# Two softmax roots as one GpSimd power each, and a new instruction order, in a block-attention residual kernel

## The chip, the cores and the metric

One core of a Trainium2 chip runs the whole program. The metric is the device time of one execution in microseconds (us). The engines are PE (TensorE), DVE (VectorE), ACT (ScalarE), POOL (GpSimd) and SP (SyncE, which here only issues DMAs).

## The reference, cut to what matters

The input x has 8 batches of 512 rows of 1024 numbers. Each batch is cut into 8 blocks of 64 rows.

```python
blk   = x.reshape(8, 8, 64, 1024).sum(axis=2)             # block sums
keys  = einsum('bnh,kh->bnk', blk, Wk)
keys  = keys / sqrt(mean(keys**2) + 1e-6) * rms_weight    # the root that is changed
attn  = softmax(einsum('bnh,h->bn', keys, cond[1]))       # over the 8 blocks
p     = einsum('bn,bnh->bh', attn, blk) @ Wo.T            # one row for each batch
y     = x + p
out   = x + (y - mean(y)) / sqrt(var(y) + 1e-6) * gamma + beta
```

## The kernel before

**Tiling.** The 8 batches go through in three groups of 2, 4 and 2 (GROUPS). In a group every partition holds whole rows of x, two in a tile x of 128x2x1024, so that "row k" (0 to 31) is one 128x1024 piece: rows 0 to 7 are group 0, rows 8 to 23 group 1, rows 24 to 31 group 2. Nine units (UNITS) of 2 or 4 rows share their statistics; U0 to U7 compute theirs on POOL, U8 on the other engines.

**Steps of a group's attention.** `bs` sums blocks on PE; `col` transposes the sums on DVE; `proj n.0` multiplies by Wk and `proj n.1` by Wo on PE. `sm n` is the softmax of group n: `sq` (ACT) and `qk` (DVE) read the projection, `sdd` spreads the two sums over 8 columns, a small matmul adds them over partitions, `v` writes the variance `cv` (128x8), then comes the inverse root `ca`, the score `sc`, the maximum `mx`, the exponential `ex0` on ACT, the reciprocal `rc` and the weights `wc`. `v n w` scales the second projection by them, `p n mm` spreads it over the partitions, two copies `cp0` and `cp1` make the tile pb, and four small DMAs put rows of it into tab.

**Steps of a row.** `S` (L646, DVE) adds p to x and sums the row; `Q` (L648, ACT) gives its sum of squares. On POOL a unit's `v`, `std` and `rs` (L692, L695, L715; std and rs are powers), and `s2`, `sd2` fill a tile stat that PE transposes (`U mm`) and ACT or DVE copies to `lt`. `D` (L746, DVE) writes (gamma + std) x y into one of three pairs of PSUM banks (t0, t1, t2), `R` (L732, PE, two rows in one step) adds the terms that depend on mean, beta and p there, and `E` (L761, ACT) scales the pair by rs back into x, which frees it for the third D after it. Each pair of rows is then stored, 1 MB; the last four rows go out singly.

**The root before.** `inverse_root` takes a logarithm (`ln`) and an exponential (`ex`) on ACT and then a Newton step: `n1` on POOL (on DVE in group 0), `n2` and `n3` on DVE.

**The order.** All steps are collected in a list with their dependences, and the string ORDER is the order in which they are emitted, with the engine (a, b, c after a step's number) and the PSUM bank (after the colon) of each. Engines run their own instructions in that order. Words like f1:7 emit matmuls of zeros that fill a bank ahead of a D or keep PE busy; z and h words add zeros to a bank in use. x and the weights are loaded through 14 tile slots on SP's queue in the order of LOADS, gamma (`gam`) behind group 1's rows.

Of the kernel before, what the change touches and what calls it, by code (L numbers as in the profile page):

```python
# [130 lines left out]
def block_attn_resid_kernel(  # L131
# [91 lines left out]
    umv = [alloc(f"umv{i}", [P, MAXU, 2]) for i in range(NU)]  # L223
    ubn = alloc("ubn", [P, 2, 2, 6])
    pmv = [alloc(f"pmv{i}", [P, 4]) for i in range(2)]
    kw = alloc("kw", [P, QU], BF16) if junk is None else junk[:, :QU]
# [5 lines left out]
        [alloc(f"{n}{i}", [P, MAXU]) for i in range(NU)] for n in ("ussq", "uv", "u0", "ua", "urs", "usx", "ustd")  # L232
# [213 lines left out]
    def project(G, which):  # L446

        n = G["n"]
        b = blkT[n % 2]
        name = f"proj{n}.{which}"  # L450
        w = wT[which].rearrange("p c (q j k) -> p c j q k", j=4, k=HB)
        if (n, which) in PARTS:
            at = 0
# [450 lines left out]
```

## Time and profile before

| | |
|---|---|
| median of 3 runs | 146.02 us (145.58 to 146.04) |
| profiled execution | 144.9 us |
| its span, first to last instruction | 143.2 us |
| mean granted TensorE clock | 0.932 |
| busy: PE, DVE, ACT, POOL | 78%, 67%, 64%, 41% |
| moved by DMA | 42.76 MB, 299 GB/s over the span |

The profiled execution is 1.7 us longer than its span and 1.1 us shorter than the median. The shares are means over stages with different limits, so they have to be read stage by stage: loading and group 0 up to 56 us, the attention of group 1 up to 73.6 us, then the rows up to 138 us and the last stores.

### The profile page before, as it was taken

Reading aid. Unit: us, or ns where it says so; the run is one execution under the profiler, and the core shown is the slowest. Engines: PE = TensorE matmul, PEld = TensorE weight load, DVE = VectorE, ACT = ScalarE, POOL = GpSimd, SP = SyncE. Lnnn points to the kernel's source line nnn. Section 1 sums busy time; section 2 is a strip of 40 time slices with the busy share of each in tenths; the row PEclk is TensorE's granted clock in tenths of the full one; section 3 lists DMA queues with packets and bytes.
Section 4 is the critical chain, followed back from the end, with each engine's and each line's share of the span. In section 5 each row is a group of like instructions: output and inputs, shape, how many; then the busy total and the mean of one; then the engine's idle time right before and its main releaser. Section 6 shows DMA issues by size and latency. Waiting matters only on the chain.

```text
span 143.2 us, 2871 instructions
## 1 busy us (share of the span) xinstructions
PE 112.3 (78%) x1093; PEld 58.9 (41%) x1101; DVE 95.5 (67%) x161; ACT 90.9 (64%) x140; POOL 58.5 (41%) x107
## 2 busy tenths in 40 slices
PE   7869853989999685999693989989798498496820
PEld 2539652947985222544340335443252132122300
DVE  3040312311315996928879999999999999997930
ACT  3022520024931898255689989899989989989630
POOL 6888800000000066652000895566506928809100
PEclk9995999599999999999999599999999869999965
DMA  4999999999999999605499870724770850775993
GB/s 126 427 413 422 413 409 414 410 411 423 426 410 424 410 413 420 263 0 238 204 307 417 314 295 5 293 89 204 291 298 6 347 240 0 295 293 220 411 401 145
DMA packets 7526, 42.76 MB, mean 299 GB/s; under 512 B 808, under 2 KB 808, under 8 KB 3672
## 3 DMA queue, kind: packets, MB, share of 16 engines
q1 hardware_dynamic: 7440, 42.54, 73.5%
q8 instruction: 8, 0.13, 0.4%
q10 hardware_dynamic: 72, 0.04, 0.1%
q14 instruction: 6, 0.05, 0.1%
HBM read 25.73 MB, written 16.78 MB: 297 GB/s over the span
## 4 chain that ended last, share of the span: by engine, by line
DMA 33%; PE 24%; DVE 17%; ACT 11%; issue 6%; POOL 3%; SPq 2%; DVEq 0%; ACTq 0%
PE b L473 11%; DVE t L746 9%; DMA gam<-in_L_cond_ln_gamma_dram 8%; DMA x<-in_L_cond_Wo_dram 8%; DMA x<-in_L_cond_Wk_dram 6%; DMA x<-in_x_dram 5%; PE t L732 5%; PE t L407 4%; ACT x L761 4%; DVE x L646 4%; ACT square L648 3%; DMA tab<-in_L_cond_ln_gamma_dram 3%; DMA pb<-in_cond_dram 3%; ACT woT L241 2%; PE b L429 1%
## 5 line engine op out<-in xcount | busy, mean ns | idle before, releaser
L746 DVE SCALAR_TENSOR_TENSOR t<-gam,ustd,x 128x1024 f32<-128x1024 f32 x31 | 39.1, 1291 | 3.7 <-ACT x L761 2.5
L648 ACT ACTIVATE square<-x,tot 128x1024 bf16<-128x1024 f32 x32 | 36.7, 1147 | 3.3 <-DVE x L646 2.1
L646 DVE SCALAR_TENSOR_TENSOR x<-x,pb 128x1024 f32<-128x1024 f32 x32 | 37.6, 1223 | 0.1
L761 ACT ACTIVATE x<-t,urs 128x1024 f32<-128x1024 f32 x31 | 33.2, 1107 | 5.5 <-PE t L732 2.4
L700 POOL TENSOR_SCALAR stat<-tot 128x8 f32<-128x8 f32 (+1 forms) x8 | 7.5, 934 | 53.1 <-DVE x L646 53.0
L732 PE MATMUL t<-tab,lt 32*128 32x512 f32 x124 | 24.9, 667 | 4.8 <-DVE lt L243 2.2
L407 PE MATMUL t<-ident,x 128*128 128x128 f32 x120 | 17.9, 316 | 5.3 <-DMA x<-in_L_cond_Wk_dram 3.0
L869 PE MATMUL b<-zeros 128*128 128x512 bf16 (+1 forms) x57 | 18.2, 439 | 2.1 <-DVE zeros L294 1.0
L407 PEld LDWEIGHTS t<-ident,x 128*128 128x128 f32 x120 | 16.9, 202 | 6.6 <-issue 4.7
L869 PEld LDWEIGHTS <-zeros 128*128 128x128 bf16 x87 | 8.7, 108 | 17.2 <-issue 12.8
L695 POOL TENSOR_TENSOR ustd<-uv,halfs 128x4 f32<-128x4 f32 (+1 forms) x8 | 13.3, 1660 | 5.5 <-DVE uv L692 4.1
L732 PEld LDWEIGHTS t<-tab,lt 32*128 32x128 f32 x124 | 7.5, 191 | 16.9 <-DVE t L746 5.7
L241 ACT COPY wkT<-t 128x1024 f32<-128x1024 f32 x5 | 5.1, 1013 | 14.1 <-PE t L407 14.1
L715 POOL TENSOR_TENSOR urs<-uv,halfs 128x4 f32<-128x4 f32 (+1 forms) x8 | 13.2, 1650 | 0.0
L243 DVE COPY wkT<-t 128x1024 f32<-128x1024 f32 x3 | 3.7, 1225 | 12.1 <-PE t L407 12.1
L429 PE MATMUL b<-x,blk 128*32 128x256 f32 x128 | 8.4, 384 | 4.2 <-DMA x<-in_x_dram 3.7
L473 PE MATMUL b<-wkT,blkT 128*32 128x256 f32 x192 | 11.0, 380 | 0.6 <-DVE blkT L439 0.6
L241 ACT COPY woT<-t 128x1024 f32<-128x1024 f32 x6 | 5.8, 1014 | 7.8 <-PE t L407 7.8
L429 PE MATMUL t<-x,blk 128*32 128x256 f32 x128 | 7.9, 382 | 3.1 <-DMA x<-in_x_dram 3.1
L473 PEld LDWEIGHTS b<-wkT,blkT 128*32 128x32 f32 x192 | 5.9, 110 | 5.8 <-issue 1.2
L473 PE MATMUL b<-woT,blkT 128*32 128x256 f32 x128 | 7.9, 382 | 0.0
L869 PE MATMUL t<-zeros 128*128 128x512 bf16 x22 | 6.4, 380 | 1.1 <-ACT lt L241 0.6
(94 smaller groups left out, 101.8 us busy)
## 6 DMA issues: line engine op xcount, KB each, us to landing
x<-in_x_dram SPq DMA_DIRECT2D x16, 1024.0 KB
out_dram<-x SPq DMA_DIRECT2D x14, 1024.0 KB
x<-in_L_cond_Wk_dram SPq DMA_DIRECT2D x4, 1024.0 KB
x<-in_L_cond_Wo_dram SPq DMA_DIRECT2D x3, 1024.0 KB
out_dram<-x SPq DMA_DIRECT2D x3, 512.0 KB
x<-in_L_cond_Wo_dram SPq DMA_DIRECT2D x2, 512.0 KB
gam<-in_L_cond_ln_gamma_dram SPq DMA_DIRECT2D x1, 512.0 KB
out_dram<-x SPq DMA_DIRECT2D x2, 256.0 KB
```

Source lines behind the costliest of these rows:

```text
L241: nc.scalar.copy(dst, src)
L407: nc.tensor.transpose(half(part, c // 4)[:, bass.ts(c % 4, P)], tile_of(name)[:, e % RT, c::HC], ident)
L429: nc.tensor.matmul(bank(f"bs{n}")[32 * j : 32 * j + 32, :QU], blk[G["g"]], tile_of(name)[:, r, bass.ts(j, QU)], start=(t == 0 and r == 0), ...
L473: nc.tensor.matmul(bank(name)[32 * j : 32 * j + 32, :QU], b[:, c, :], w[:, c, j], start=(c == 0), stop=(c == HC - 1),)
L646: add(f"S{k}", [(DVE, 1.15)], lambda e: nc.vector.scalar_tensor_tensor(x_row(k), x_row(k), 1.0, pb[n], ALU.mult, ALU.add, accum_out=total) ...
L648: add(f"Q{k}", [(ACT, 1.28)], lambda e: nc.scalar.activation(square, x_row(k), AF.Square, bias=total, scale=-float(H), accum_out=ssq), rea ...
L695: add(f"{T} std", [(POOL, 0.5 + 0.16 * U)], lambda e: nc.gpsimd.tensor_tensor(std, v, halfs[:, :1].to_broadcast([P, U]), ALU.pow), reads=[ ...
L715: add(f"{T} rs", [(POOL, 0.5 + 0.16 * U)], lambda e: nc.gpsimd.tensor_tensor(rs, v, halfs[:, 1:].to_broadcast([P, U]), ALU.pow), reads=[V, ...
L732: nc.tensor.matmul(half(f"row{k}", h), lts[q % NST][lo : lo + 32, r // RT, :], tab_of(k)[0][lo : lo + 32, :], start=False, stop=True, skip ...
L746: add(f"D{k}", [(DVE, 1.21)], lambda e: nc.vector.scalar_tensor_tensor(flat(pair(name)), gam, std, x_row(k), ALU.add, ALU.mult), reads=["g ...
L761: add(f"E{k}", [(ACT, 1.13)], lambda e: nc.scalar.activation(x_row(k), flat(pair(name)), AF.Identity, scale=rs), reads=[RS], writes=[xk(k) ...
L869: nc.tensor.matmul(bank_at(i)[:, :n], zeros, zeros[:, 0:1].to_broadcast([P, n]), start=start, stop=True, skip_group_check=True)
```

## The change

In groups 1 and 2 the five steps of the inverse root become one step `pow` on POOL: cv to the power -0.5, a 128x8 tensor against a constant of -0.5. Group 0 keeps the old root. Beside this, scratch tiles are shared: `diag` and the scratch output `kw` (bf16 before) become parts of the tile vw0 (f32), and the tiles u0 and ua, which only U8 uses, exist once. The other new branches of the code (kinds "a" and "d", BY_PE, DIVIDE) are not taken with the constants given. ORDER is new as a whole.

```diff
+ROOT_POW = (1, 2)
+DIVIDE = False
 ORDER = (
-    "0 2 3 65:0 1 104 4 66:1 95 5 110 67:2 6 99 7 68:3 103 8 9 10 11 12 13 14 15 17 16 18 19 20 21 22 23 24 f11:7 "
+    "1 3 65:0 95 2 4 104 66:1 100 5 0 112 67:2 6 97 7 68:3 8 9 10 11 12 13 14 15 17 16 18 19 20 21 22 23 24 f11:7 "
...
-    diag = alloc("diag", [P, 32])
...
+    diag = vw[0][:, :32]
...
-    kw = alloc("kw", [P, QU], BF16) if junk is None else junk[:, :QU]
+    kw = vw[0]
...
-            reads=["qw"], writes=["sd1"], use=keys)
+            reads=["qw"], writes=["sd1", "vw0"], use=keys)
...
-        inverse_root(T, cv, c0, ca, ca, ("cv", "c0", "ca", "ca"))
+        if n in ROOT_POW:
+            add(f"{T} pow", [(POOL, 2.0)], lambda e: nc.gpsimd.tensor_tensor(
+                ca, cv, halfs[:, 1:].to_broadcast([P, NBLK]), ALU.pow), reads=["cv", "halfs"], writes=["ca"])
+        else:
+            inverse_root(T, cv, c0, ca, ca, ("cv", "c0", "ca", "ca"))
```

Three places show how the order moves. The first is DVE in the softmax of group 1, from the variance to the first rows of group 1 (x12, x13); before:

```order
L507 TENSOR_SCALAR cv_123<-b0_82 128x8
L746 SCALAR_TENSOR_TENSOR t1_80<-gam_102,ustd1_155,x6_69 128x1024
L487 SCALAR_TENSOR_TENSOR ca_126<-ca_126,cv_123 128x8
L489 SCALAR_TENSOR_TENSOR ca_126<-ca_126,c0_125 128x8
L510 SCALAR_TENSOR_TENSOR cs_124<-b0_82,ca_126 128x8
L512 TENSOR_REDUCE mx_127<-cs_124 128x1
L746 SCALAR_TENSOR_TENSOR t2_81<-gam_102,ustd1_155,x6_69 128x1024
L243 COPY lt1_104<-b0_82 128x256
L515 RECIPROCAL es_128<-es_128 128x1
L516 SCALAR_TENSOR_TENSOR kw_120,wcol_129<-cs_124,es_128,diag8_90 128x8
L746 SCALAR_TENSOR_TENSOR t0_79<-gam_102,ustd1_155,x8_71 128x1024
L746 SCALAR_TENSOR_TENSOR t1_80<-gam_102,ustd1_155,x8_71 128x1024
```

and the same place of the change, one row further down:

```order
L798 SCALAR_TENSOR_TENSOR t1_80<-gam_101,ustd1_136,x6_69 128x1024
L523 SCALAR_TENSOR_TENSOR cs_115<-b0_82,ca_117 128x8
L525 TENSOR_REDUCE mx_118<-cs_115 128x1
L798 SCALAR_TENSOR_TENSOR t2_81<-gam_101,ustd1_136,x6_69 128x1024
L529 RECIPROCAL es_119<-es_119 128x1
L530 SCALAR_TENSOR_TENSOR vw0_106,wcol_120<-cs_115,es_119,diag8_89 128x8
L544 TENSOR_SCALAR vw0_106<-b1_83,wcol_120 128x256
L798 SCALAR_TENSOR_TENSOR t0_79<-gam_101,ustd1_136,x8_71 128x1024
L252 COPY pb1_108<-b0_82 128x4x128
L692 SCALAR_TENSOR_TENSOR x12_75,tot0_96<-x12_75,pb1_108 128x1024 x2
L798 SCALAR_TENSOR_TENSOR t1_80<-gam_101,ustd1_136,x8_71 128x1024
```

The two Newton steps and the copy of lt1 are gone from DVE; the scaling of vw0 and one half of pb1, which ACT did, have come to it; and the last D of group 0 (row 7, x8 into t1) stands behind the first two S of group 1.

The second place is POOL around the softmax of group 2; before (ca is the Newton product, uv0, ustd0 and stat0 belong to unit U4):

```order
L501 TENSOR_TENSOR sdd_122<-diag8_90,sd_121 128x16
L700 TENSOR_SCALAR stat0_95<-tot0_97 128x8
L486 TENSOR_TENSOR ca_126<-c0_125 128x8
L692 TENSOR_SCALAR uv0_134<-ussq0_130 128x4
L695 TENSOR_TENSOR ustd0_154<-uv0_134,halfs_87 128x4
L715 TENSOR_TENSOR urs0_146<-uv0_134,halfs_87 128x4
L710 TENSOR_TENSOR stat0_95<-ustd0_154,ind4_100 128x8x5
```

and with the change:

```order
L752 TENSOR_SCALAR stat0_94<-tot0_96 128x8
L510 TENSOR_TENSOR sdd_113<-diag8_89,sd_112 128x16
L519 TENSOR_TENSOR ca_117<-cv_114,halfs_87 128x8
L743 TENSOR_SCALAR uv0_125<-ussq0_121 128x4
L746 TENSOR_TENSOR ustd0_135<-uv0_125,halfs_87 128x4
L762 TENSOR_TENSOR stat0_94<-ustd0_135,ind4_99 128x8x5
L767 TENSOR_TENSOR urs0_131<-uv0_125,halfs_87 128x4
```

The power stands where the Newton product stood, ahead of U4's own variance and powers, on which the D of row 16 waits.

The third place is ACT near the end, from the last Q on; before:

```order
L648 ACTIVATE square_112,ussq0_130<-x4_67,tot0_97 128x1024
L761 ACTIVATE x9_72<-t1_80,urs2_148 128x1024
L484 ACTIVATE u00_138<-uv0_134 128x2
L485 ACTIVATE u00_138<-u00_138 128x2
L761 ACTIVATE x11_74<-t2_81,urs2_148 128x1024
L761 ACTIVATE x11_74<-t0_79,urs2_148 128x1024
L241 COPY lt1_104<-b0_82 128x128
```

and with the change:

```order
L813 ACTIVATE x10_73<-t0_79,urs2_133 128x1024
L694 ACTIVATE square_111,ussq0_121<-x4_67,tot0_96 128x1024
L742 ACTIVATE uv0_125<-ussq0_121,least_88 128x2
L493 ACTIVATE u00_129<-uv0_125 128x2
L813 ACTIVATE x11_74<-t2_81,urs2_133 128x1024
L494 ACTIVATE u00_129<-u00_129 128x2
L813 ACTIVATE x11_74<-t1_80,urs2_133 128x1024
```

The E of row 25 now stands ahead of the last Q (x4, row 31) and no longer behind it, U8's variance has come to ACT, and U7's lt copy has gone to DVE.

## Rows read from the trace of the kernel before

**Rows 1.** Stages: window, length, busy us of PE, PEld, DVE, ACT, POOL; clock, DMA share, GB/s.

```profile
56.14:73.64 17.50, 15.72 (x191) 7.29 (x194) 12.88 (x23) 9.97 (x20) 5.31 (x5) 1.00 0.54 200
73.64:97.00 23.36, 19.43 (x230) 8.81 (x227) 23.02 (x38) 21.66 (x36) 13.24 (x13) 0.93 0.61 248
...
110.00:128.00 18.00, 13.38 (x56) 4.58 (x56) 17.97 (x26) 16.88 (x24) 11.44 (x10) 0.91 0.57 234
```

**Rows 2.** Timeline of DVE, group 1's softmax: start, duration, instruction, [idle before].

```profile
56.14 0.69 DVE L352 TENSOR_SCALAR gam<-gam 128x1024 f32<-128x1024 f32 x1 [1.10 <-DMA gam<-in_L_cond_ln_gamma_dram]
...
62.50 0.42 DVE L498 SCALAR_TENSOR_TENSOR kw<-b,qw 128x256 bf16<-128x256 f32 x1 [1.74 <-ACT square L496]
...
65.39 0.16 DVE L507 TENSOR_SCALAR cv<-b 128x8 f32<-128x8 f32 x1
...
67.51 0.17 DVE L510 SCALAR_TENSOR_TENSOR cs<-b,ca 128x8 f32<-128x8 f32 x1
...
68.38 1.29 DVE L746 SCALAR_TENSOR_TENSOR t<-gam,ustd,x 128x1024 f32<-128x1024 f32 x1 [0.51 <-ACT x L761]
69.58 0.42 DVE L243 COPY lt<-b 128x256 f32<-128x256 f32 x1
69.91 0.15 DVE L515 RECIPROCAL es<-es 128x1 f32<-128x1 f32 x1
...
72.44 1.29 DVE L746 SCALAR_TENSOR_TENSOR t<-gam,ustd,x 128x1024 f32<-128x1024 f32 x1 [0.89 <-ACT x L761]
73.64 1.22 DVE L646 SCALAR_TENSOR_TENSOR x<-x,pb 128x1024 f32<-128x1024 f32 x1
```

**Rows 3.** Timeline of ACT: group 1's two pb copies; the E of rows 10 and 11.

```profile
72.30 1.06 ACT L241 COPY pb<-b 128x512 f32<-128x512 f32 x2
...
93.00 2.12 ACT L761 ACTIVATE x<-t,urs 128x1024 f32<-128x1024 f32 x2 [0.51 <-PE t L732]
```

**Rows 4.** Timeline of POOL: the Newton products, and powers of 4 and 2 columns.

```profile
66.11 0.89 POOL L486 TENSOR_TENSOR ca<-c 128x8 f32<-128x8 f32 x1 [3.27 <-ACT c L485]
...
96.94 0.20 POOL L486 TENSOR_TENSOR ca<-c 128x8 f32<-128x8 f32 x1 [1.40 <-ACT c L485]
...
98.39 1.97 POOL L695 TENSOR_TENSOR ustd<-uv,halfs 128x4 f32<-128x4 f32 x1
...
129.08 0.72 POOL L695 TENSOR_TENSOR ustd<-uv,halfs 128x2 f32<-128x2 f32 x1 [4.14 <-DVE uv L692]
```

**Rows 5.** Timeline of DVE from group 2's softmax on.

```profile
96.97 1.29 DVE L746 SCALAR_TENSOR_TENSOR t<-gam,ustd,x 128x1024 f32<-128x1024 f32 x1 [0.32 <-PE t L869]
98.17 0.16 DVE L487 SCALAR_TENSOR_TENSOR ca<-ca,cv 128x8 f32<-128x8 f32 x1
98.25 1.22 DVE L646 SCALAR_TENSOR_TENSOR x<-x,pb 128x1024 f32<-128x1024 f32 x1
...
106.62 0.69 DVE L243 COPY pb<-b 128x512 f32<-128x512 f32 x1
107.22 1.22 DVE L646 SCALAR_TENSOR_TENSOR x<-x,pb 128x1024 f32<-128x1024 f32 x1
```

**Rows 6.** Timeline of PE: the fills ahead of group 1's projection; 32 matmuls of group 2's second one.

```profile
57.24 1.03 PE L869 MATMUL t<-zeros 128*128 128x512 bf16 x4 [0.32 <-DVE blkT L439]
...
92.89 1.93 PE L473 MATMUL b<-woT,blkT 128*32 128x256 f32 x32
```

**Rows 7.** The end: ACT's E of rows 25, 26 and 27; SP's store of rows 24 and 25; DMA by windows.

```profile
128.62 1.10 ACT L761 ACTIVATE x<-t,urs 128x1024 f32<-128x1024 f32 x1
...
129.96 2.10 ACT L761 ACTIVATE x<-t,urs 128x1024 f32<-128x1024 f32 x2
...
129.75 0.33 SPq L813 DMA_DIRECT2D out_dram<-x  x1
...
130.00:131.00 1.00, 0.89 (x6) 0.45 (x5) 1.00 (x1) 1.00 (x3) 0.97 (x2) 1.00 0.57 238
...
140.00:141.00 1.00, 0.00 (x0) 0.00 (x0) 0.00 (x0) 0.00 (x0) 0.00 (x0) 0.50 0.87 334
```

More of the change, by code (lines that the diff above doesn't have):

```diff
@@ L231, in block_attn_resid_kernel @@
     ussq, uv, u0, ua, urs, usx, ustd = (
[L232 removed]
+        [alloc(f"{n}{i}", [P, MAXU]) for i in range(k)] * (NU // k) if k else [None] * NU for n, k in (
+            ("ussq", NU), ("uv", NU), ("u0", 1), ("ua", NU if "b" in UKIND else 1), ("urs", NU),
+            ("usx", NU if set(UKIND) & set("pa") else 0), ("ustd", NU))
     )
@@ L388, in table @@
                 out=t[32 * q + 2 : 32 * q + 2 + g, :], in_=p[0:P:w, i * HALF : (i + 1) * HALF]),
-                reads=[f"pb{n % 2}.{j}" for j in range(2)], writes=[f"tab{n % NTAB}.{q}"], mb=0.01)
+                reads=[f"pb{n % NPB}.{j}" for j in range(2)], writes=[f"tab{n % NTAB}.{q}"], mb=0.01)
         if (n, "x") in TABS:
@@ L464, in project @@
                     add(f"{name}.{at}.{c0}.{qs}.{cs}", [(PE, 0.012 * cs + 0.108 * qs * cs)], lambda e, go=go: go(),
-                        reads=[f"blkT{n % 2}"] + w_keys(which, range(2 * at, 2 * (at + qs)), halves[0]),
+                        reads=[f"blkT{n % NBT}"] + w_keys(which, range(2 * at, 2 * (at + qs)), halves[0]),
                         claim=("b", name) if at == c0 == 0 else None, use=[] if at == c0 == 0 else [name])
@@ L477, in project @@
             add(f"{name}.{c0}", [(PE, 0.98)], lambda e, go=go: go(),
-                reads=[f"blkT{n % 2}"] + w_keys(which),
+                reads=[f"blkT{n % NBT}"] + w_keys(which),
                 claim=None if c0 else ("b", name), use=[name] if c0 else [])
@@ L536, in spread_out @@
             add(f"{part} cp{i}", [(ACT, 0.6), (DVE, 0.69)], lambda e, i=i: copy(
-                e, bands(pb[n % 2])[:, :, i, :], half(part, i).rearrange("p (q d) -> p q d", d=P)),
-                reads=[("slot", part)], writes=[f"pb{n % 2}.{i}"], release=part)
+                e, bands(pb[n % NPB])[:, :, i, :], half(part, i).rearrange("p (q d) -> p q d", d=P)),
+                reads=[("slot", part)], writes=[f"pb{n % NPB}.{i}"], release=part)
     def spread_p(G, part, start):
@@ L644, in moments, with go @@
                 reads=[S], writes=[Q], use=y, release=[y, y])
+        elif kind in "ad":
+            if place[k][1] % RT == 0:
+                tile_ = x_name(k)
+                add(f"A{k}", [(POOL, ADD_ISSUE)], lambda e: nc.gpsimd.dma_start(
+                    out=tile_of(tile_), in_=pb[n].unsqueeze(1).to_broadcast([P, RT, H]), accum_op=ALU.add),
+                    reads=p_keys, writes=[xk(k), xk(k + 1)], mb=ADD_MB)
+            if kind == "a":
+                add(f"Q{k}", [(ACT, 1.34)], lambda e: nc.scalar.activation(
+                    square, x_row(k), AF.Square, bias=total, scale=-float(H), accum_out=ssq), reads=[xk(k), S], writes=[Q])
+            else:
+                b = ubn[:, k % 2]
+                add(f"B{k}", [(DVE, 1.3)], lambda e: both_halves(b, x_row(k)), reads=[xk(k)], writes=[f"ubn{k % 2}"])
+                add(f"C{k}", [(DVE, 0.2)], lambda e: nc.vector.bn_aggr(out=umv[u][:, r, :], in_=b),
+                    reads=[f"ubn{k % 2}"], writes=[f"umv{u}.{r}"])
+        elif k in BY_PE:
+            y = f"y{k}"
+            def go():
+                for h in range(2):
+                    nc.tensor.matmul(pair(y)[:, h, :].rearrange("p (q d) -> p q d", d=P), ident, bands(x_row(k))[:, :, h, :],
+                                     start=True, stop=False, skip_group_check=True)
+                spread_p(G, y, False)
+            add(f"Y{k}", [(PE, 2.75)], lambda e: go(), reads=["ident", xk(k), "vw0", f"spread{g}"], claim=("t", y))
+            add(f"V{k}", [(ACT, 1.3)], lambda e: nc.scalar.activation(
+                bands(x_row(k)).rearrange("p q i d -> p i q d"), pair(y).rearrange("p i (q d) -> p i q d", d=P),
+                AF.Identity, accum_out=total), writes=[xk(k), S], use=y, release=[y, y])
+            add(f"Q{k}", [(ACT, 1.28)], lambda e: nc.scalar.activation(
+                square, x_row(k), AF.Square, bias=total, scale=-float(H), accum_out=ssq), reads=[xk(k), S], writes=[Q])
         else:
@@ L685, in unit @@
                 a, umv[u][:, :U, 1], UP * UP, pmv[n][:, 2:3], ALU.mult, ALU.add),
-                reads=[f"umv{u}.{r}" for r in range(U)] + [f"pmv{n}.2"], writes=[f"ua{u}"])
+                reads=[f"umv{u}.{r}" for r in range(U)] + [f"pmv{n}.2"], writes=[A])
             add(f"{T} vc", [(E, c)], lambda e: engine[e].tensor_scalar(v, ssq, 2.0 / H * UP * UP, 0.0, ALU.mult, ALU.add),
                 reads=Q4, writes=[V])
-            add(f"{T} v", [(E, c)], lambda e: engine[e].tensor_tensor(v, v, a, ALU.add), reads=[f"ua{u}"], writes=[V])
+            add(f"{T} v", [(E, c)], lambda e: engine[e].tensor_tensor(v, v, a, ALU.add), reads=[A], writes=[V])
+        elif UKIND[q] == "d":
+            add(f"{T} v", [(E, c), (DVE, 0.18)] if slow else [(E, c)], lambda e: engine[e].tensor_scalar(
+                v, umv[u][:, :U, 1], UP * UP, EPS * UP * UP, ALU.mult, ALU.add),
+                reads=[f"umv{u}.{r}" for r in range(U)], writes=[V])
         else:
```

74 lines of the change are left out of this document (43 added, 31 removed), and 40 rows, old and new, of the table ORDER.

## The prediction

> **What bounds the kernel now.** I read the windows by stage first, then the timelines of DVE, ACT and POOL in the stages that the change touches, then the end. Up to 56 us the kernel loads; the stage ends with DVE idle for 1.10 us until gamma has landed [rows 2]. From there to 73.64 us DVE is busy 12.88 us of 17.50 and PE 15.72 [rows 1]: the softmax of group 1 is a chain through PE and ACT, and DVE waits in it, 1.74 us before `qk`, 0.51 and 0.89 us before two D [rows 2]. From 73.64 us on DVE has hardly a gap: 23.02 us busy of 23.36, 17.97 of 18.00, with ACT at 21.66 and 16.88 [rows 1]. Here a microsecond of DVE work is a microsecond of time. At the end DMA takes over: the store of rows 24 and 25 is issued at 129.75 us, when their last E (128.62, 1.10 long) is done; the DMA engines are at work from about 130.4 us (0.57 of the window from 130 to 131) to about 140.9 (0.87 of that from 140) [rows 7]. The stores from there on are 4 MB, 4.19 million bytes in 10.5 us or 0.4 MB per us, so they run without a pause. The store of rows 26 and 27 can be issued when its E ends at 129.96 + 2.10 = 132.06, and the MB ahead of it is through at about 130.4 + 2.5 = 132.9; with the 0.65 us from issue to first bytes that 129.75 and 130.4 show, it comes 0.15 us ahead of its turn. A later E of row 27 by d moves the end by d - 0.15.
>
> **The root itself.** In group 1 the old root runs from the end of `cv`, 65.55, to `sc` at 67.51, 1.96 us [rows 2]. But `sc` and the maximum feed the exponential, which stands on ACT behind an E; the D that waits for the same E starts only at 68.38 [rows 2], and that E waits for PE. A shorter root gains nothing there, and a longer one costs nothing before about 68.2. In group 2 DVE works rows while the root is under way: what leaves DVE is two Newton steps at 98.25 - 98.17 = 0.08 us each, start to start [rows 5], so -0.16; on ACT `ln` and `ex` go, which is not the bound.
>
> The power of 128x8 is in no row. From below it is bounded by the shortest power, 0.72 us for 2 columns; from above by twice the longest of 4 columns shown, 2 x 1.97 = 3.94 [rows 4]. What its row shows is a wait and a calculation: the power issued at 98.39 ends at 100.36, and the S that DVE ran from 98.25 ended at 99.47 [rows 4, 5], so 0.9 us lie behind that S. The same is seen in the two Newton products, one operation and one shape: 0.89 us with a D running on DVE, 0.20 in a gap of DVE [rows 4, 5]. From 0.72 for 2 columns and 0.9 for 4, I take 0.09 a column, 1.3 us for 8, after the end of the D or S that is running. The Trainium skill, in "SBUF — State Buffer", section "Who interferes with whom", says that a DVE instruction with two SBUF inputs and a GpSimd instruction that reads SBUF exclude each other, and that the one that comes second is blocked entirely. The 0.89 against 0.20 us agree, and by that rule the move to POOL costs a wait that a count of columns would not show; without it the wait at D16 below would fall away and the sum would be 146.3.
>
> **Where this counts.** In group 2 the new order has `cv` at about 97.0 (below) and D14 straight behind it on DVE, so the power waits until 98.2 and ends at about 99.6. Behind it on POOL are U4's variance and `std`, and D16 needs that `std`. The variance slips in when S21 ends, 100.6; `std` waits for D15, 101.75, and takes 0.9: 102.7. DVE is ready for D16 at 102.05. So 0.7 us of waiting if the power takes more than about 1.1 us, none if less; I take 0.5.
>
> **The order, group 1.** The loads keep their sequence, and what moves before 56 us is covered by the 1.10 us wait for gamma (if that cover were gone, whatever the weight copies that change engine lose beyond 1.10 us would count in full). PE: two of the four fills from 57.24 on, 1.03 us together [rows 6], go from ahead of the projection to behind it, so D2, whose bank they fill, waits for them: 57.24 + 0.5 for the two that stay, some 3.8 for 64 matmuls at 1.93 for 32 [rows 6], and 0.5 for the two, 62.0. `qk` follows at 63.2 where it was 62.50 [rows 2], but the small matmul stands behind a projection step that ends no earlier than 64.0, and `cv` comes at 64.4 where it was 65.39, as a D no longer precedes it. The power then ends at 67.2, in time. So the spread matmul ends just before 72.30 as it did: its two copies, one behind the other on ACT from 72.30 for 1.06 us [rows 3], now run side by side on DVE and ACT, and S8 starts at 72.9, not 73.64. But D7, which was done at 73.64 (72.44 + 1.20) [rows 2], is now behind S9: 72.9 + 1.20 - 73.64 = **+0.45 us** of DVE work behind the old state.
>
> **The order, rows.** Moves between DVE and ACT, start to start: U2's `lt` copy to DVE +0.33 (69.58 to 69.91) [rows 2]; half of group 2's pb to ACT -0.60 (106.62 to 107.22) [rows 5]; the Newton steps -0.16. The wait of 0.32 us for a fill at 96.97 [rows 5] goes, as the new order has that fill elsewhere: -0.32. New waits: the step R of rows 10 and 11 still follows the first projection, so E10 starts near 93.0 as before [rows 3] and frees D12's bank at 94.15, when DVE, with S19 and `qk` done earlier, is ready at 93.85: +0.3. D13's fill is on PE behind 32 projection matmuls of 1.93 us [rows 6] that begin at 93.35, so 95.3 plus a fill, 95.55 against 95.35: +0.2. D16: +0.5. In sum 0.45 + 0.33 - 0.60 - 0.16 - 0.32 + 0.3 + 0.2 + 0.5 = **+0.70 us** at D27.
>
> **The end.** E26 follows the step R behind D27, and U8's `ex` now stands between E26 and E27, 0.2 us: E27 is +0.9, and with the 0.15 of slack the end +0.75. The half of row 31 that goes from DVE to ACT and the U7 and U8 steps that change engine come after D27 and only have to keep ahead of the DMA queue, which has 2 MB in it by then. All of this is made against the profiled execution: 144.9 + 0.75 = 145.65. The median of the runs is 1.12 above that execution, and the forecast is 146.02 + 0.75, rounded to 146.8.
>
> **Rivals.**
> 1. No change. The power takes 1.1 us or less, D16 does not wait, and the new waits at D12 and D13 come to 0.3 together: 0.70 - 0.5 - 0.2 = 0.0, with E27 within the slack: 146.0. For it: the root is hidden in both groups, so the change proper is worth nothing on the path. Against: three POOL instructions in a row each meet a running D or S.
> 2. Faster. The rows are paced by ACT's E rather than by DVE, and ACT is early: S8 at 72.9 lets Q8 start 0.74 us earlier, and ACT loses two `ln`, two `ex` and a pb copy. Then the end comes 0.7 earlier: 145.3. For it: D waits for E in [rows 2]; against: DVE is busy 98 to 99% of the rows' stages [rows 1]. It decides if the D of group 1's rows are found waiting for E.
> 3. Slower still, by POOL. U2, U5 and U6 reach their `std` by my reckoning only 0.2 us before their D asks for it. If two of these miss by one DVE instruction, the blocked read comes 1.2 us later, of which 0.2 is cover: +2 x 1.0, less 0.5 if D16's wait then does not come: 146.8 + 1.5 = 148.3; one of them alone 147.8.
>
> **Chances.** Forecast (146.3 to 147.4) 0.43, of which 0.06 is within 0.3%; rival 1, 0.22; rival 2, 0.25; rival 3, 0.10. About 0.3%, 0.44 us, is what a measurement of this kernel can tell from no change. Faster 0.25, same 0.22 + 0.06 = 0.28, slower 0.37 + 0.10 = 0.47. The range reaches from most of rival 2 to the lower part of rival 3: 145.1 to 147.7; the likeliest case has 146.3 to 147.4.
>
> **What would show it.** The power at 0.9 to 1.5 us behind the end of a D in both groups; S8 at about 72.9 and D7 behind S9; a wait of D16 for POOL's `std`; E27's end 0.9 us later than 132.06 and DMA without a pause from there to the end. The forecast is wrong if DVE's idle time in the rows' stage does not grow, if S8 starts before 72.5, or if E25 and E27 both end earlier than before.

## The result, and the profile after

The changed kernel takes 149.69 us (median of 4 runs, 148.59 to 153.48) against 146.03 for the kernel before beside it: ratio 1.0275, 95% interval 1.0233 to 1.0318. Some executions of most kernels here come out more than 1.5% above the fastest one; the medians contain them, the ratios leave them out, and no time is read from a profile that caught one. The sign was forecast, the size was not: 0.75 us expected, about 4.0 measured by the ratio (3.7 between the medians), and 147.7, the upper end of the range, is passed. The profiled execution took 149.54 us, its span is 147.8 (143.2 before), its mean granted clock 0.907 (0.932 before).

The stages of the change by windows, cut as in [rows 1] where the new order allows it; the columns are those of [rows 1]:

```profile
56.17:73.17 17.00, 14.30 (x175) 6.39 (x177) 12.41 (x21) 8.34 (x14) 7.44 (x6) 1.00 0.52 203
73.17:99.00 25.83, 22.33 (x243) 9.57 (x245) 24.88 (x38) 22.64 (x35) 13.26 (x13) 0.93 0.61 244
112.00:130.00 18.00, 15.42 (x60) 4.82 (x59) 17.66 (x22) 17.93 (x27) 12.61 (x12) 0.87 0.57 233
130.00:138.00 8.00, 4.77 (x22) 1.67 (x22) 4.90 (x10) 4.77 (x8) 4.23 (x4) 0.79 0.33 133
```

The last window is new: from 130 to 138 us DVE is busy 4.90 us of 8, and DMA moves 133 GB/s, where before it ran without a pause from 130.4 [rows 7]. DVE's timeline shows the waits one by one (start, duration, instruction, idle before):

```profile
56.17 0.69 DVE L361 TENSOR_SCALAR gam<-gam 128x1024 f32<-128x1024 f32 x1 [0.95 <-DMA gam<-in_L_cond_ln_gamma_dram]
...
67.32 0.17 DVE L523 SCALAR_TENSOR_TENSOR cs<-b,ca 128x8 f32<-128x8 f32 x1 [0.32 <-POOL ca L519]
...
73.17 1.23 DVE L692 SCALAR_TENSOR_TENSOR x<-x,pb 128x1024 f32<-128x1024 f32 x1
...
75.47 1.29 DVE L798 SCALAR_TENSOR_TENSOR t<-gam,ustd,x 128x1024 f32<-128x1024 f32 x1
...
86.57 0.42 DVE L252 COPY lt<-b 128x256 f32<-128x256 f32 x1 [0.54 <-PE b L773]
...
94.97 2.64 DVE L798 SCALAR_TENSOR_TENSOR t<-gam,ustd,x 128x1024 f32<-128x1024 f32 x2 [0.32 <-POOL sdd L510]
...
103.39 1.39 DVE L798 SCALAR_TENSOR_TENSOR t<-gam,ustd,x 128x1024 f32<-128x1024 f32 x1 [0.64 <-POOL ustd L746]
...
112.34 1.29 DVE L798 SCALAR_TENSOR_TENSOR t<-gam,ustd,x 128x1024 f32<-128x1024 f32 x1 [0.81 <-ACT x L813]
...
133.46 0.29 DVE L252 COPY lt<-b 128x128 f32<-128x128 f32 x1 [0.50 <-PE b L773]
136.09 1.29 DVE L798 SCALAR_TENSOR_TENSOR t<-gam,ustd,x 128x1024 f32<-128x1024 f32 x1 [2.35 <-ACT x L813]
```

In order these are gamma, the score of group 1, S8, D7, U2's lt, D12, D16, D19, U7's lt and D29. If the starts of the same S and D in the two timelines are set side by side, the delay grows like this:

| up to | before | after | behind | added here | forecast of it |
|---|---|---|---|---|---|
| S10 (group 1's softmax) | 75.92 | 76.67 | 0.75 | 0.75 | 0.45 |
| D10 (U2's lt) | 85.56 | 87.28 | 1.72 | 0.97 | 0.33 |
| D15 (Newton, fills, D12, D13) | 99.47 | 101.21 | 1.74 | 0.02 | 0.02 |
| D16 | 100.95 | 103.39 | 2.44 | 0.70 | 0.50 |
| S23 (half of pb to ACT) | 107.22 | 109.16 | 1.94 | -0.50 | -0.60 |
| S25 (D19's wait) | 110.70 | 113.54 | 2.84 | 0.90 | 0 |
| D27 | 127.63 | 130.48 | 2.85 | 0.01 | 0 |
| end of E27 | 132.06 | 137.15 | 5.09 | 2.24 | 0.20 |

The largest term is at the end. PE's and ACT's rows there, two timelines one behind the other:

```profile
133.09 0.33 PE L773 MATMUL b<-ident,stat 128*128 128x128 f32 x1 [2.90 <-POOL stat L762]
133.35 1.58 PE L784 MATMUL t<-tab,lt 32*128 32x512 f32 x8
```

```profile
134.94 1.11 ACT L813 ACTIVATE x<-t,urs 128x1024 f32<-128x1024 f32 x1 [2.32 <-PE t L784]
135.96 0.19 ACT L494 ACTIVATE u<-u 128x2 f32<-128x2 f32 x1
136.05 1.10 ACT L813 ACTIVATE x<-t,urs 128x1024 f32<-128x1024 f32 x1
```

In the kernel before, R of rows 26 and 27 stood ahead of that transpose; PE's rows there:

```profile
127.77 2.33 PE L732 MATMUL t<-tab,lt 32*128 32x512 f32 x8 [0.21 <-DVE t L746]
130.16 0.33 PE L721 MATMUL b<-ident,stat 128*128 128x128 f32 x1
```

With the change D27 is done at 131.8, but R of rows 26 and 27 (133.35) starts only behind the transpose of U7's stat (133.09), which belongs to rows 28 and 29 and now stands ahead of it on PE. So ACT waits 2.32 us for E26. POOL's timeline shows when the stat comes:

```profile
97.88 2.63 POOL L519 TENSOR_TENSOR ca<-cv,halfs 128x8 f32<-128x8 f32 x1 [2.94 <-DVE cv L516]
100.60 0.73 POOL L743 TENSOR_SCALAR uv<-ussq 128x4 f32<-128x4 f32 x1
101.42 1.94 POOL L746 TENSOR_TENSOR ustd<-uv,halfs 128x4 f32<-128x4 f32 x1
...
128.20 1.07 POOL L743 TENSOR_SCALAR uv<-ussq 128x2 f32<-128x2 f32 x1
129.36 1.58 POOL L746 TENSOR_TENSOR ustd<-uv,halfs 128x2 f32<-128x2 f32 x1
130.92 1.39 POOL L767 TENSOR_TENSOR urs<-uv,halfs 128x2 f32<-128x2 f32 x1
132.28 0.75 POOL L762 TENSOR_TENSOR stat<-ustd,ind 128x20 f32<-128x20 f32 x1
```

U7's variance, before one of two small operations of DVE that took 0.23 us together, takes 1.07 us on POOL beside running S and D, and rs now stands ahead of stat. But measured from D27 the stat is no later than it was: its transpose starts 2.61 us behind the start of D27 (133.09 and 130.48), before 2.53 (130.16 and 127.63). What is new is that R stands behind it. The first three rows are the root of group 2 and U4 behind it. The transfers show what the late E27 does, windows of 1 us (the last two columns are DMA's share and GB/s):

```profile
134.00:135.00 1.00, 0.93 (x8) 0.13 (x2) 0.00 (x0) 0.06 (x1) 0.00 (x0) 0.50 0.28 115
135.00:136.00 1.00, 0.74 (x2) 0.29 (x2) 0.00 (x0) 1.00 (x2) 0.00 (x0) 0.50 0.00 0
136.00:137.00 1.00, 1.00 (x3) 0.15 (x1) 0.91 (x1) 1.00 (x3) 0.77 (x1) 0.50 0.00 0
137.00:138.00 1.00, 1.00 (x9) 0.64 (x8) 0.78 (x4) 0.16 (x1) 0.43 (x1) 0.83 0.00 0
138.00:139.00 1.00, 0.83 (x7) 0.16 (x2) 0.96 (x3) 0.57 (x1) 0.00 (x0) 1.00 1.07 451
```

DMA stands still for between three and four microseconds until the store of rows 26 and 27 is issued. 5.09 us less the 0.15 of slack would be 4.9; the span grew by 4.6.

### The profile page after: what moved, and what is told of

The parts are those of the page before. It is cut to its first block, busy times and chain, and to the rows that moved or that the text cites. A ratio compares the mean times of both kernels' runs of the same rounds, so it can differ in the third digit from the quotient of the medians.

```text
span 147.8 us, 2846 instructions
## 1 busy us (share of the span) xinstructions
PE 116.1 (79%) x1086; PEld 57.9 (39%) x1095; DVE 98.5 (67%) x159; ACT 88.2 (60%) x132; POOL 64.2 (43%) x109
## 4 chain that ended last, share of the span: by engine, by line
DMA 33%; PE 29%; DVE 14%; POOL 11%; ACT 4%; issue 4%; POOLq 1%; SPq 0%; DVEq 0%; ACTq 0%
PE b L482 12%; DMA gam<-in_L_cond_ln_gamma_dram 10%; DMA x<-in_L_cond_Wo_dram 7%; PE t L784 6%; DMA x<-in_L_cond_Wk_dram 6%; DVE t L798 5%; DMA x<-in_x_dram 5%; DVE x L692 4%; PE t L416 4%; POOL ustd L746 4%; DMA pb<-n_L_cond_rms_weight_dram 3%; DMA tab<-in_L_cond_ln_gamma_dram 3%; POOL urs L767 2%; ACT x L813 2%; PE b L559 2%
## 5 line engine op out<-in xcount | busy, mean ns | idle before, releaser
L921 PE MATMUL b<-zeros 128*128 128x512 bf16 (+1 forms) x53 | 19.3, 487 | 3.5 <-DVE zeros L303 2.1
L416 PE MATMUL t<-ident,x 128*128 128x128 f32 x120 | 16.9, 301 | 4.2 <-DMA x<-in_L_cond_Wk_dram 2.6
L416 PEld LDWEIGHTS t<-ident,x 128*128 128x128 f32 x120 | 15.9, 199 | 5.4 <-issue 4.8
L746 POOL TENSOR_TENSOR ustd<-uv,halfs 128x4 f32<-128x4 f32 (+1 forms) x8 | 14.9, 1868 | 0.7
L438 PE MATMUL b<-x,blk 128*32 128x256 f32 x128 | 9.2, 415 | 4.9 <-DMA x<-in_x_dram 4.1
L250 ACT COPY wkT<-t 128x1024 f32<-128x1024 f32 x4 | 4.0, 1014 | 15.1 <-PE t L416 15.1
L252 DVE COPY wkT<-t 128x1024 f32<-128x1024 f32 x4 | 4.8, 1222 | 11.8 <-PE t L416 11.8
L250 ACT COPY woT<-t 128x1024 f32<-128x1024 f32 x4 | 4.0, 1008 | 8.1 <-PE t L416 7.9
L743 POOL TENSOR_SCALAR uv<-ussq 128x4 f32<-128x4 f32 (+1 forms) x8 | 6.0, 744 | 5.4 <-ACT square L694 5.3
L921 PE MATMUL t<-zeros 128*128 128x512 bf16 x19 | 7.4, 479 | 1.0 <-DVE blkT L448 0.7
```

Source lines behind the costliest of these rows:

```text
L250: nc.scalar.copy(dst, src)
L416: nc.tensor.transpose(half(part, c // 4)[:, bass.ts(c % 4, P)], tile_of(name)[:, e % RT, c::HC], ident)
L438: nc.tensor.matmul(bank(f"bs{n}")[32 * j : 32 * j + 32, :QU], blk[G["g"]], tile_of(name)[:, r, bass.ts(j, QU)], start=(t == 0 and r == 0), ...
L746: add(f"{T} std", [(POOL, 0.5 + 0.16 * U)], lambda e: nc.gpsimd.tensor_tensor(std, v, halfs[:, :1].to_broadcast([P, U]), ALU.pow), reads=[ ...
L921: nc.tensor.matmul(bank_at(i)[:, :n], zeros, zeros[:, 0:1].to_broadcast([P, n]), start=start, stop=True, skip_group_check=True)
```

## The experiments

Ratios are to the kernel before, run beside each experiment (145.06 to 145.94 us in the median), with the 95% interval. No time is read from the profiles of root_only, mid_after, b_acts_pow and tail_r26. Numbers in ORDER are steps; the diffs show the words around a join.

### Which part of the change costs: the root or the order

**root_only**: the order of before, the power in both groups.

```diff
-255 226:2 256 207 257 258b 208 269 259 260 261
+255 226:2 207 256 208 265 257
...
-h3:6 f1:4 322 326:4 401 333 402b 403 361 323 340a 341 404
+h3:6 f1:4 318 322:4 329 396 357 319 336a 337
```

> The order of before with the new power at the place where the Newton product stood on POOL, in groups 1 and 2; tiles shared as in the change. Theory order (the 4 us come from the new instruction order): 145.9 to 146.4 us, since the power has the place of a product that was not on the path, DVE loses two Newton steps (0.16 us), and in group 2 the power starts at the S boundary near 96.6, ends near 97.9 and so is clear of U4's variance, which waits for a Q until 98.0. Theory power (the longer stay on POOL is itself the cost): 147 us or more, with D16 waiting for POOL's std by 0.5 us or more and the score of group 1 waiting for the power.

Measured 146.43 us, ratio 1.0064 (1.0030 to 1.0097). The time lies just above the first theory's range, and the reason given for "no cost" was wrong: in all six profiles read here that have the power ahead of U4's std, in either order, D16 waits 0.63 or 0.64 us for std.

**order_only**: the new order with the old root.

```diff
-ROOT_POW = (1, 2)
+ROOT_POW = ()
...
-206:0 256 264 204 226:2 207 257
+206:0 256 257 258b 268 204 226:2 207 259 260 261
```

> The new order with the old root (logarithm, exponential, Newton step) put in where the power stood. Theory order: 149.0 us, that is the time of the change less the wait of 0.64 us that D16 has for std behind the power, plus 0.16 for the two Newton steps on DVE. Theory power: 146.0 to 146.6.

Measured 149.84, ratio 1.0290 (1.0224 to 1.0356). The new order has the whole loss without the power, too; no gain from taking the power out can be seen within the interval. POOL's Newton product took 1.23 us beside a D there, and D16 still waited 0.26 us.

**root1_only**: the order of before, the power in group 1, the old root in group 2.

```diff
-ROOT_POW = (1, 2)
+ROOT_POW = (1,)
```

> The order of before; the power in group 1 only, the old root in group 2. Theory U4 (the root's cost is POOL's: in group 2 the power makes U4's variance and std each miss a DVE boundary, so that D16 waits 0.6 us): ratio to before 1.000, within 0.002, and D16 follows D15 without a wait. Rival (the power costs in group 1, or the shared tiles cost): 1.004 to 1.008, as with the power in both groups (1.0064).

Measured 145.84, ratio 1.0016 (0.9975 to 1.0058). In group 1 the power and the shared tiles cost nothing that can be measured (the interval reaches to 0.6%); D16 has no wait.

### Which piece of the new order costs

Three kernels join the two orders at the S of row 15 (step 307) or of row 27 (step 420), all with the power in both groups.

**front_after**: new, then old.

```diff
-235 307 286 236 f6:7 385 289:4 308 237 285 290:0
+235 307 236 285 237 289:4 311 f8:7 f1:1 385 308
```

> The new order up to the S of row 15 (about 82 us), then the order of before, with the power in both groups. Theory ledger (DVE is the bound of the rows, so what group 1's softmax leaves behind stays): S10 0.75 us later than before, the same 0.75 at D8 and at D27, the end 0.6 later: 146.6 us. Rival (the rows have slack on DVE and take the delay back): 146.0. Rival (the delay upsets what follows, clock or waits): 147.5 or more.

**tail_after**: old, then new from the S of row 27 on.

```diff
-354 419 376:0 f4:7 372 417 420 373 441 424 421 377:4 374
+371:0 369a 419 376:2 f3:7 372 415 420 373 441 424 421 377:4 374
```

> The order of before with the power in both groups up to the S of row 27 (about 119 us), then the new order's end (banks t0 and t1 exchanged to fit). Theory tail: R26 waits behind U7's transpose, E26 2.3 us later than with the old end, on top of the 0.9 us that the power costs: 3.2 us over before, ratio 1.020 to 1.024. Rival (the end of the program takes it back, as the transfers are what ends last): 1.006 to 1.010.

**mid_after**: old, new between the two joins, old.

```diff
+303 235 282a 305 283 236 307 302 286 f6:7 385 289:4
...
+372 417 420 373 441 424 421 377:4 442 422a 443 423 374 f7:7 378
```

> The order of before up to the S of row 15, the new order from there to the S of row 27, then the old end; the power in both groups. Theory ledger: of the 2.87 us by which the change is behind at D24, 0.75 are group 1's softmax and 2.1 are made here (U2's copy 0.97, D16's wait 0.64, the rest around D19), and the old end adds nothing: ratio 1.013 to 1.016. Rival (those waits come from the delay that group 1 hands on, not from the order here): 1.004 to 1.008.

Measured: front_after 146.37, ratio 1.0081 (1.0056 to 1.0107); tail_after 147.87, 1.0170 (1.0113 to 1.0228); mid_after 147.61, 1.0134 (1.0079 to 1.0189). Each holds the power's 0.0064. Beyond it the front costs 0.0017, the middle 0.0070 and the end 0.0106; with the power they sum to 0.0257, against 0.0275 for the whole change. So the price is spread over the middle and the end. Which of the two is larger these runs don't settle, as their intervals overlap; and the sum is a rough one, since in order_only the loss was as large without the power. tail_after came out below its forecast (1.020 to 1.024), the other two as their first theories said. In front_after's profile the delay is 0.80 us at S10, 0.53 at D15 and 1.24 at D16, with this row of DVE at D16:

```profile
102.19 1.29 DVE L798 SCALAR_TENSOR_TENSOR t<-gam,ustd,x 128x1024 f32<-128x1024 f32 x1 [0.64 <-POOL ustd L746]
```

At D27 it is 1.42 (129.05 and 127.63): DVE takes nothing back.

### The end: one step on PE

**r26_first**: the change, with U7's transpose (450) behind R of rows 26 and 27 (437).

```diff
-452:0 f4:7 450:6 437 463b 451b 464 438 465 453:4
+452:0 f4:7 437 463b 450:6 464 438 451b 465 453:4
```

> The change with one step moved on PE: the transpose of U7's stat behind the matmuls R of rows 26 and 27. Theory tail (R26 waits for U7's stat from POOL only because it stands behind it on PE): E26 starts near 132.9 instead of 134.94, E27 ends near 135.1 instead of 137.15, the store of rows 26 and 27 goes 2 us earlier and the end with it: 147.6 us. Rival (U8's chain and the last rows set the end, not rows 26 and 27): below 0.5 us of gain, 149.2 or more.

Measured 148.50, ratio 1.0260 (1.0189 to 1.0330). E26 starts 1.89 us after D27 (133.35 and 131.46), not 4.46 as in the change. But D27 itself is 0.98 later than in the change, as PE's granted clock was 0.50 to 0.52 from 84 to 90 us there and the projection late. In the profiles E27 still ends 1.61 us earlier than in the change (135.54 and 137.15) and the span is 1.6 shorter, but the ratio of all runs is hardly lower, with an interval wide enough for either theory. That left the step's price open, and two runs test it in the old order:

**tail_r26**: tail_after with the same edit. **b_u7**: the kernel before, with U7's std, stat and transpose ahead of R26 (445 in its numbers).

```diff
-444:0 441 453c f2:6 f3:7 445 471a 454 456 472 442 460:2 473 446 474b 458:6 447
+444:0 441 453c f2:6 f3:7 454 456 458:6 445 471a 472 442 460:2 473 446 474b 447
```

> As the run with the old order up to row 27 and the new end, with one step moved on PE: U7's transpose behind R of rows 26 and 27. Theory tail: of the 1.5 us (1.017 against 1.0064) that the new end costs, nearly all goes: 1.006 to 1.009, E26 1.9 us after D27 starts and not 4.5. Rival (other parts of the new end cost it, such as U7 and U8 on other engines): 1.014 or more.

> The order and the roots of before, with U7's std, stat and transpose put ahead of R of rows 26 and 27 on PE, and nothing else. Theory tail (R waits for POOL if it stands behind the transpose): the transpose ends near 130.5, R a matmul pair of 1.13 us later, E26 at 131.1 to 131.6 instead of 129.96, the end 1.0 to 1.5 later: ratio 1.007 to 1.010. Rival (the transfers in flight cover it): 1.000 to 1.003.

Measured: tail_r26 146.02, ratio 0.9979 (0.9934 to 1.0025), against 1.0170 with the transpose ahead; b_u7 147.48, ratio 1.0074 (1.0032 to 1.0116). The one step costs at either end. tail_r26 even lies below its forecast and below the old end with the power (root_only, 1.0064): with the power in place, the new end without that step is better than the old one. PE and ACT of b_u7:

```profile
130.22 0.33 PE L773 MATMUL b<-ident,stat 128*128 128x128 f32 x1 [2.66 <-POOL stat L762]
130.48 1.14 PE L784 MATMUL t<-tab,lt 32*128 32x512 f32 x8
```

```profile
131.65 2.12 ACT L813 ACTIVATE x<-t,urs 128x1024 f32<-128x1024 f32 x2 [1.54 <-PE t L784]
```

D27 starts at 127.69, almost as before; the transpose comes at 130.22, E26 at 131.65, where it was 129.96. The step seems to have a second price. In the three profiles where PE stood still for 2.66 to 2.90 us ahead of this transpose (the change, tail_after, b_u7), the granted clock fell to 0.50 within two microseconds of the end of that pause, at about 133.9, 132.4 and 131.9 us, and R of rows 28 and 29 then took 1.47, 2.12 and 2.25 us, before 1.29. In the kernel before, r26_first and more_fills the clock is 1.00 from 130 to 136 us. No run separates the two prices.

### The middle: PE's clock, U2's transpose, the power's place

**more_fills**: r26_first with more zeros at three places.

```diff
-236 f6:7 385
+236 f12:7 385
...
-h2:7 z5:4 324
+h2:7 z9:4 324
...
-443 f6:7 378
+443 f9:7 378
```

> The change with U7's transpose behind R of rows 26 and 27, and more matmuls of zeros on PE at three places where its clock drops to half behind a pause: 12 for 6 ahead of the last block sum of group 2, 9 for 5 ahead of R of rows 14 and 15, 9 for 6 ahead of R of rows 22 and 23. Theory clock (PE at half clock makes U2's copy wait 0.54 and, through R of rows 16 and 17, D19 0.81): granted clock 1.0 from 82 to 86 and from 103 to 113 us, both waits gone, 1.3 us less than with the transpose moved alone, ratio 1.015 to 1.018 against 1.026. Rival (the clock is not what these waits hang on, or the zeros themselves delay what follows): 1.024 or more.

Measured 147.10, ratio 1.0115 (1.0067 to 1.0163), better than the forecast. The gain on r26_first is not made at D19, which waits in neither profile. D27 comes at 129.57, where it was 131.46: from 84 to 88 us the clock is 1.00 here, so `qk` doesn't wait for the projection (0.76 us in r26_first) and D12 waits 0.32 us and not 1.24. U2's copy still waits 0.60 us, and three things make this wait: when x lands, PE's clock and the order of its steps. PE's last block sum of group 2, which needs the last x tile, and the three matmuls of zeros stand ahead of U2's transpose; in the change and in order_only, one behind the other:

```profile
83.04 1.94 PE L438 MATMUL b<-x,blk 128*32 128x256 f32 x16 [2.36 <-DMA x<-in_x_dram]
84.91 1.41 PE L921 MATMUL t<-zeros 128*128 128x512 bf16 x3
```

```profile
83.15 1.07 PE L438 MATMUL b<-x,blk 128*32 128x256 f32 x16 [2.40 <-DMA x<-in_x_dram]
84.15 0.82 PE L921 MATMUL t<-zeros 128*128 128x512 bf16 x3
```

With x there at the same time and the same zeros, the copy waits 0.54 us in the change, at a clock of 0.50, and not at all in order_only, at 1.00. In more_fills the clock is 1.00 too, but the block sum waits for x until 84.50.

Now to D19. PE in the changed kernel (spread matmul of group 2, R of rows 16 and 17), then in more_fills:

```profile
107.00 2.08 PE L559 MATMUL b<-vw,spread 64*128 64x256 f32 x8 [0.73 <-DVE vw L544]
109.01 2.09 PE L784 MATMUL t<-tab,lt 32*128 32x512 f32 x8
```

```profile
107.01 1.13 PE L559 MATMUL b<-vw,spread 64*128 64x256 f32 x8 [1.35 <-DVE vw L544]
108.07 1.17 PE L784 MATMUL t<-tab,lt 32*128 32x512 f32 x8
```

They start alike and take 4.1 us at the lower level (granted clock 0.50, 1.2 GHz), 2.2 at the upper (1.00, 2.4 GHz). Over the five profiles of this order's middle the wait goes with the level: 0.81, 0.67 and 0.80 us at D19 in the change, order_only and u2_first (R 2.09, 1.94 and 2.09 us long), none in r26_first and more_fills (1.17 both). No run sets the level by itself, so this is read from the chain (spread matmul, R, E16, D19) and not shown by an edit.

**u2_first**: more_fills with U2's transpose (287) ahead of the three matmuls of zeros.

```diff
-306 f3:3 287:7 288b 386
+306 287:7 f3:3 288b 386
```

> The change with U7's transpose behind R of rows 26 and 27, with more zeros as in the run before, and with U2's transpose ahead of the three matmuls of zeros that stand before it on PE (86.17 us there). Theory PE order: those zeros make DVE's copy of U2's lt wait 0.54 to 0.60 us; with them behind it the wait is 0 and D10 0.55 earlier: ratio 1.007 to 1.009 against 1.0115. Rival (the load of the last x tile of group 2, which the block sum ahead of both waits for, sets it): wait unchanged, 1.010 to 1.013.

Measured 146.85, ratio 1.0102 (1.0067 to 1.0137). The copy follows D9 at once, and D10 starts 1.90 us after D9 where it was 2.59: 0.69 gained there. But in this profile PE's clock fell to 0.50 again, at a place that had been at 1.00 in the run before with the same work ahead of it, and D19 waited 0.80 us; so the local gain is shown, a gain in time is not (1.007 to 1.009 was forecast). PE and DVE:

```profile
103.63 0.44 PE L773 MATMUL b<-ident,stat 128*128 128x128 f32 x2
104.72 1.36 PE L921 MATMUL t<-zeros 128*128 128x512 bf16 x3 [0.65 <-DVE t L798]
106.88 2.08 PE L559 MATMUL b<-vw,spread 64*128 64x256 f32 x8 [0.80 <-DVE vw L544]
```

```profile
112.22 1.29 DVE L798 SCALAR_TENSOR_TENSOR t<-gam,ustd,x 128x1024 f32<-128x1024 f32 x1 [0.80 <-ACT x L813]
```

**pow_late**: u2_first with the power (396) behind U4's variance and std (336, 337), score and maximum (397, 398) behind S22, and D17 (344) ahead of the reciprocal and the weights.

```diff
-396 355 319 320 357 336a 337 356 321 323:2 339 358 397 h2:7 z9:4 324 398 343:0 340 341:6 399 359
+355 319 320 357 336a 337 396 356 321 323:2 339 358 h2:7 z9:4 324 343:0 340 341:6 359 397 398
```

> As the one with U2's transpose first, and in group 2 the power behind U4's variance and std on POOL, with score, maximum and the steps behind them later on DVE (after S22). Theory POOL (the power costs only because U4's std stands behind it): no wait of D16, and D17 at the same place after it: 0.64 us less than with U2's transpose first, ratio about 1.004. Rival (the later score delays the spread matmul, the copies of pb and E of row 16, and D19 waits for it instead): no gain.

Measured 146.85, ratio 1.0043 (1.0000 to 1.0086). POOL:

```profile
97.91 0.42 POOL L743 TENSOR_SCALAR uv<-ussq 128x4 f32<-128x4 f32 x1 [3.69 <-ACT square L694]
98.42 1.89 POOL L746 TENSOR_TENSOR ustd<-uv,halfs 128x4 f32<-128x4 f32 x1
100.29 1.77 POOL L519 TENSOR_TENSOR ca<-cv,halfs 128x8 f32<-128x8 f32 x1
```

std ends at 100.31 and D16 follows D15 without a wait. D19 waits 0.43 us in this profile, where R of rows 16 and 17 takes 1.62 us and the clock falls from 1.00 to 0.50 while it runs. With the four edits together (U7's transpose, the zeros, U2's transpose, the power) the new order is at 1.0043, where the change is at 1.0275. Most of its loss lies at these places, though the runs don't price each of them alone.

### Towards a faster kernel

**b_acts**: the kernel before with one half of pb and U6's lt given to ACT. **b_acts_pow**: the same with the power, late in group 2. **best_old**: the old order and roots up to row 27, then the new end as in tail_r26. **best_acts**: best_old with the half of pb on ACT.

```diff
-349 360 417b 350 365 416a 354:2
+349 360 350 365 416a 417a 354:2
...
-384 436b 469
+384 436a 469
```

> The order and the roots of before, with two copies given from DVE to ACT: one half of group 2's pb and U6's lt. Theory DVE (DVE is the bound of the rows, ACT has room): 0.60 and 0.33 us less on DVE, row 25 and the end 0.9 earlier, ratio 0.994. Rival (ACT is as near: its later E hold up D): 0.999 to 1.003.

> As the last one, with the power in groups 1 and 2, in group 2 behind U4's std, with the score after S22 and R of rows 16 and 17 ahead of the spread matmul. Theory POOL: D16 does not wait, two Newton steps leave DVE (0.16 us): equal to the last one or 0.1 to 0.2 us faster, ratio 0.993. Rival (the later score is paid at D19 or S24): 0.998 or more.

> The order and the roots of before up to the S of row 27, then the new end with U7's transpose behind R of rows 26 and 27. Theory (the power's cost at D16 and the place of U7's transpose are two separate prices): 0.6 us less than with the power, D27 no later than in before, ratio 0.992 to 0.995. Rival (the power's 0.6 us is taken back by this end): 0.997 to 0.999, as with the power.

> As the last one, with both halves of group 2's pb copied by ACT. Theory DVE: 0.60 us less on DVE, no E so late that a D waits for it before the end: ratio 0.988 to 0.992. Rival (ACT's E are late by then, as where two copies were given to it): equal to the last one.

Measured: b_acts 145.39, ratio 1.0004 (0.9978 to 1.0030); b_acts_pow 146.69, 1.0055 (1.0021 to 1.0089); best_old 145.36, 0.9970 (0.9938 to 1.0003); best_acts 145.19, 0.9976 (0.9938 to 1.0013). In b_acts DVE is 0.40 us ahead at D22 and gives it back at D27:

```profile
127.98 1.29 DVE L798 SCALAR_TENSOR_TENSOR t<-gam,ustd,x 128x1024 f32<-128x1024 f32 x1 [0.91 <-ACT x L813]
```

There ACT is as near as DVE: the rival held. b_acts_pow, best_old and best_acts all came out above their first forecasts (0.993, 0.992 to 0.995 and 0.988 to 0.992); in best_old D27 starts at 128.26, 0.63 us later than before, and not earlier. None of these beats the kernel before beyond its interval. That best_old equals tail_r26 says that at this end 0.6 us of DVE no longer reach the time, or are too small to see beside the intervals; the runs don't tell which.

## Why the prediction was wrong in its size

**The step that failed** is the last one before the rivals: that the U7 and U8 steps that change engine "come after D27 and only have to keep ahead of the DMA queue". U7's transpose stands ahead of R of rows 26 and 27 on PE, so these rows wait for POOL's stat of other rows. 2.24 us are added there, 0.20 were forecast. Taking the step out of the new end brought the ratio from 1.0170 to 0.9979, putting it into the old end made 1.0074. In the change itself the ratio hardly moved when the step was taken out (1.0260 for 1.0275). The prediction followed ACT's queue at the end and not PE's.

**The second** is the sum of the rows, which took PE's lengths from rows at a clock of 1.00 and had no term for a lower one. Its -0.60 for the pb half came, as -0.50, and was lost again at D19. There E16 follows a spread matmul and an R that run at the lower clock level (0.50 from 106 to 112 us), and E16 is late: +0.90, where 0 was forecast. The sum also took each microsecond of DVE in the rows for a microsecond of time. b_acts took two copies off DVE, 0.60 and 0.33 us, and the time did not move beyond its interval; D27 waited 0.91 us for ACT there.

**Third, U2's lt.** The 0.33 for the copy was right. The 0.54 of waiting came from the order of PE's steps and from its clock together: a block sum and three matmuls of zeros stand ahead of U2's transpose, and from the start of that sum to the transpose it was 3.1 us at the lower level, 1.8 in order_only at the upper. With the transpose ahead of the zeros the wait goes (u2_first), and at the upper level it goes too (order_only).

**Fourth, group 1.** The mechanism was right: S8 earlier, D7 behind S9, `cv` and the end of the power within 0.1 us of the forecast. But S8 came at 73.17, not 72.9: the copy of pb started at 72.39 and S8 0.78 later, where 0.6 had been taken. That makes 0.75 for 0.45.

**What held.** The loads: gamma's wait is 0.95 us, and nothing before 56 us counts. The root is hidden in group 1 (root1_only). The terms of Newton, fills, D12 and D13 sum to 0.02 as forecast. D12 has its 0.32 us wait for E10: the row names POOL's `sdd`, but D12 starts 0.1 us behind the end of E10 both here and in r26_first, where `sdd` had ended 0.9 us before. The size is in part luck, as E10 and DVE both came 0.7 to 0.8 us later than reckoned. D16 waits 0.64 us for std behind the power, forecast 0.5, and front_after and tail_after have the same wait where their order is the old one. The power ended 1.6 us behind the end of the D that ran beside it (98.91 to 100.51), not 1.3. That POOL's power, variance and std each waited for an instruction of DVE to end was the mechanism of this term. It agrees with the rule that the prediction took from the Trainium skill's "SBUF — State Buffer", section "Who interferes with whom". E27 was to be 0.9 us later and DMA to run on: E27 was 5.09 later, and DMA paused for more than 3 us. Rival 3 named POOL's missed boundaries as the way to a larger loss, at U2, U5 and U6; the loss came at U7, through PE.

## What to carry to other kernels

When an order is rewritten, read each engine's queue at every place where a step of another unit has moved ahead of the critical one, PE's small transposes too: a step of 0.33 us put ahead of R made E26 1.7 us later in one order and 2.6 in the other, by a wait for an engine that nobody counted. A small operation moved to POOL beside DVE work should be priced by the ends of DVE's instructions that it has to wait for and by who stands behind it in POOL's queue, not by its own length. Look at PE's clock level in the rows from which a length is taken. Add the delays along the engine that is the bound, and check the last link, where the store of the last rows decides whether DMA keeps running.

## What was not expected of the hardware

The granted clock falls at different places in executions whose steps are nearly the same. In more_fills and u2_first PE's rows from 97.4 to 104.8 us start 0.12 to 0.14 us apart and are otherwise alike, and the window from 106 to 108 us was at 1.00 in one and 0.50 in the other:

```profile
106.00:108.00 2.00, 0.99 (x8) 0.76 (x8) 1.86 (x5) 1.24 (x2) 0.00 (x0) 1.00 0.70 295
```

```profile
106.00:108.00 2.00, 1.20 (x7) 1.03 (x8) 1.89 (x5) 1.12 (x2) 0.00 (x0) 0.50 0.79 328
```

In both PE had paused for 0.65 us ahead of the zeros at 104.7 to 104.8. The Trainium skill, in "TensorE: Matmul & The Clock Gate", section "🔬 Part 1: The HAM clock gate (the "warmup" mystery)", says that the gate's window runs freely and does not start with the kernel. That would fit two outcomes of one sequence, but no run here shows the window itself. Whether a low stretch costs anything depends on what stands there: from 113 to 117 us in the kernel before no D waited for it, at 107 to 111 in the new order it cost 0.8 us.
